# A WKV-scan block on one core: spreads and scans share one pool of eleven tiles, the decay's exponential moves from PSUM to SBUF, TensorE gets eight PSUM banks

## The chip, the cores and the metric

The kernel runs on one core of a Trainium2 chip. The metric is the device time of one execution in microseconds; several executions are timed and their median is the kernel's time. The core has five engines with a queue of instructions each: TensorE (PE; its weight loads are shown as PEld), VectorE (DVE), ScalarE (ACT), GpSimd (POOL) and SyncE (SP), which here issues most of the DMAs. Each engine works its own queue strictly in order, and semaphores hold an instruction until what it needs is done. SBUF is the large on-chip memory, PSUM the small one in which TensorE leaves its results; in this kernel GpSimd only ever reads and writes SBUF.

## What is computed

`x` has 8 batches of 256 tokens with 512 channels. Each batch goes through one recurrent block, all in float32:

```python
xn = ln(x); sx = shift(xn) - xn                                  # token shift
xxx = tanh((xn + sx * maa_x) @ maa_w1)                           # five small gates
x5  = xn + sx * (maa_stack + xxx @ maa_w2)                       # five mixed inputs
w = exp(-exp(time_decay + tanh(x5[1] @ decay_w1) @ decay_w2))
r, k, v = x5[3] @ Wr.T, x5[0] @ Wk.T, x5[2] @ Wv.T
g = silu(x5[4] @ Wg.T)
for t in tokens:                                                 # 32 heads of 16 x 16 state
    a = k_t[:, None] * v_t[None, :]
    out_t = r_t @ (u * a + s)
    s = a + w_t[:, None] * s
x = x + (groupnorm(out) * g) @ Wo.T
xn2 = ln2(x); sx2 = shift(xn2) - xn2
x = x + sigmoid(xr @ ffn_Wr.T) * (relu(xk @ ffn_Wk.T) ** 2 @ ffn_Wv.T)   # xk, xr from xn2, sx2
```

## The kernel before

Each batch has three stages: `inputs_of_scan` (layer norm, mixing, projections to r, k, v, g and the decay), `scan` (the recurrence) and `rest` (group norm, output projection and the second half). The stages of neighbouring batches are interleaved.

**The scan.** Channels are on the partitions, in 4 blocks of 128. A block's state has 16 columns per channel, worked in 4 groups of 4 columns, so there are 8 x 4 x 4 = 128 groups. Per block, ACT writes `wrep`, the decay exp(-w) repeated four times along time (L883). Per group:

1. a DMA on the SP queue spreads `v` rows from DRAM (`vo`) into a `vs` tile of 128 x 4 x 256 (L389, 512 KB);
2. ACT writes the initial state into column 0 (L893);
3. DVE multiplies `vs` in place by `k` (L900). The copy of `k` that it reads, `kp`, was put into PSUM by ACT. For 6 of the 128 groups POOL does this product instead (L897), reading `k` from SBUF;
4. DVE runs the recurrence along time with one TENSOR_TENSOR_SCAN of 1024 elements (L902): it reads `wrep` and `vs` and writes a tile `st` of a second pool, `st8`;
5. POOL multiplies `st` by `r`, in place (L905);
6. when four groups are done, PE sums them over the key index into a PSUM tile `pat` (L913), and DVE adds that to `att` (L919).

**Memory.** `vs` has 6 tiles and `st8` has 6, each 4 KB per partition, in SBUF. `wrep` is one tile in PSUM and takes two of its eight banks; the other six are the pool `ps`, through which every result of TensorE and the `kp` copies pass. In batch 0, before the first scan, two of the mixing results are put into `wrep`'s banks (`wide` in `mixed`), and DVE then sets its first column to zero again.

**Order.** Every operation is recorded with an engine and with the tiles that it reads and writes. `Plan.order` takes the operations by a written rank, the table `TURNS` (one number per operation, a row per batch and stage), gives each a tile from its pool and a planned start, and emits them by planned start. What comes out is a fixed order on each engine's queue. Plain products ("any") take the tiling of their neighbours on PE: four matmuls on 32 columns each, or one on 128 (`mul`, L400).

The two lines on which the change turns, with their operands:

```python
    w, pat = new("wrep", f"wrep{b}_{blk}"), new("ps", f"pat{b}_{blk}")
...
    dve(4 * T, [st], [w, vs], lambda w=w, vs=vs, st=st: nc.vector.tensor_tensor_scan(st(), w(), vs(), 0.0, ALU.mult, ALU.add), 2.085)
    gp(4 * T, st, [st, r], lambda m=m, st=st, r=r: nc.gpsimd.tensor_tensor(st(), st(), r()[:, m : m + 1, :].to_broadcast([P, 4, T]), ALU.mult), 1.815)
```

(shown with the reshaping of the scan's operands left out.)

Of the kernel before, what the change touches and what calls it, by code (L numbers as in the profile page):

```python
# [12 lines left out]
P = 128  # L13
# [54 lines left out]
class Plan:  # L68
# [46 lines left out]
    def stage(self):  # L115
# [224 lines left out]
def tile_rwkv_block(  # L340
# [98 lines left out]
    pool("att", 3, [P, 2 * T + 4])  # L439

    pool("vo", 3, [2, P, T], dram)
    pool("vs", 6, [P, 4, T])
    pool("rk", 2, [P, 2, T])
    pool("st8", 6, [P, 4, T])
    pool("sq", 2, [P, E])
    pool("x2", 2, [P, NT, E + 1])
    pool("o", 2, [P, E])
    pool("Ws", 4, [P, 2, E])
    pool("wrep", 1, [P, 4, T], pp)
    pool("ps", 6, [P, 2, T], pp)  # L450


    def col(name, k):
# [679 lines left out]
```

## Time and profile before

| what | value |
|---|---|
| median of 3 runs | 613.29 us (613.27 to 614.44) |
| the profiled execution | 613.54 us, of which the span of the instructions 611.7 us |
| PE busy | 599.6 us (98%) |
| DVE busy | 545.4 us (89%) |
| POOL busy | 522.3 us (85%) |
| ACT busy | 514.3 us (84%) |
| granted TensorE clock | 0.997 on average |

A row of the groups reads: line, engine, operation, what it writes <- what it reads, shapes and count, then busy time, the mean of one in ns, and the engine's idle time just before. In the timeline a row begins with the start and the duration in us, and ends with xN, the number of equal instructions merged. The waits say who sat idle, until which instruction ended, for how long in total, how many times, and the longest. In the view by windows each stretch has the busy time of every engine and in brackets the count.

### The profile page before, as it was taken

The numbers are of one execution on the slowest core, as the hardware profiler recorded it, in microseconds if no ns is written. First come the engines' busy times: TensorE is split into PE (matmuls) and PEld (weight loads), VectorE is DVE, ScalarE is ACT, GpSimd is POOL, SyncE is SP. The second block draws the span as 40 slices with busy tenths as digits, with TensorE's granted clock in tenths as the row PEclk, the third lists the DMA queues.
The fourth block names the chain that finished last, engine by engine and source line by source line (L and its number), as shares of the span: only waits on it lengthen the run. The fifth ranks groups of instructions, "written<-read, shape, count | busy, mean of one in ns | idle before, by whom it ended". The sixth has DMA issues, their size and how long they took to land.

```text
span 611.7 us, 17692 instructions
## 1 busy us (share of the span) xinstructions
PE 599.6 (98%) x7322; PEld 350.8 (57%) x7322; DVE 545.4 (89%) x489; ACT 514.3 (84%) x1172; POOL 522.3 (85%) x418
## 2 busy tenths in 40 slices
PE   8899999999999999999999999999999999999997
PEld 7576755657544764367553775455654464547464
DVE  6599999999999998899998999999999999996342
ACT  5797689999999999999999798999899789965450
POOL 2889999999899998889998999899999988978030
PEclk9899999999999999999999999999999999999999
DMA  9897777788858777958767687896786677971552
GB/s 289 276 234 170 193 185 209 193 211 195 240 157 232 195 197 234 280 137 243 198 194 213 193 249 188 207 288 165 194 244 168 186 220 208 268 227 33 186 164 91
DMA packets 52495, 124.76 MB, mean 204 GB/s; under 512 B 5824, under 2 KB 11200, under 8 KB 52416
## 3 DMA queue, kind: packets, MB, share of 16 engines
q1 hardware_dynamic: 47904, 119.39, 71.6%
q10 hardware_dynamic: 4512, 4.26, 2.2%
q8 instruction: 57, 0.93, 0.7%
q14 instruction: 22, 0.18, 0.1%
HBM read 115.25 MB, written 8.39 MB: 202 GB/s over the span
## 4 chain that ended last, share of the span: by engine, by line
PE 84%; ACT 5%; DVE 5%; POOL 3%; issue 1%; DMA 0%; ACTq 0%; DVEq 0%; POOLq 0%
PE ps L400 70%; PE ps L913 8%; PE ps L606 2%; PE ps L777 2%; POOL st L905 1%; ACT ps L720 1%; DVE st L902 1%; ACT rk L968 1%; ACT sq L968 1%; POOL g L979 1%; PE ps L855 1%; PE ps L939 0%; DMA xt<-in_x 0%; DVE mix L639 0%; DVE mix L722 0%
## 5 line engine op out<-in xcount | busy, mean ns | idle before, releaser
L902 DVE TENSOR_TENSOR_SCAN st<-wrep,vs 128x1024 f32<-128x1024 f32 x128 | 288.8, 2276 | 4.0 <-ACT wrep L883 2.1
L905 POOL TENSOR_TENSOR st<-st,r 128x1024 f32<-128x1024 f32 x128 | 254.2, 2003 | 11.7 <-DVE st L902 7.1
L900 DVE TENSOR_TENSOR vs<-vs,ps 128x1024 f32<-128x1024 f32 x122 | 143.5, 1207 | 3.0 <-ACT vs L893 3.0
L400 PE MATMUL ps<-Ws,mix 128*32 128x512 f32 (+2 forms) x864 | 115.4, 589 | 0.2 <-DVE o L1026 0.2
L400 PEld LDWEIGHTS ps<-Ws,mix 128*32 128x32 f32 (+1 forms) x864 | 37.6, 116 | 61.8 <-issue 55.7
L737 POOL TENSOR_TENSOR mix<-mix,xn 128x512 f32<-128x512 f32 x62 | 67.0, 1098 | 5.5 <-DVE mix L722 5.3
L400 PE MATMUL ps<-mix,Wv 128*32 128x256 f32 (+1 forms) x808 | 61.6, 381 | 1.8 <-DVE mix L734 1.8
L913 PE MATMUL ps<-st,con 128*32 128x256 f32 x1024 | 62.3, 380 | 0.1
L400 PE MATMUL ps<-mix,Wk 128*32 128x256 f32 (+1 forms) x904 | 60.0, 379 | 0.6 <-DVE mix L722 0.6
L400 PE MATMUL ps<-mix,Wg 128*32 128x256 f32 (+1 forms) x736 | 59.1, 380 | 0.2 <-DVE mix L722 0.2
L400 PE MATMUL ps<-mix,Wr 128*32 128x256 f32 (+1 forms) x712 | 59.0, 380 | 0.0
L400 PE MATMUL ps<-mix,Ws 128*32 128x256 f32 (+1 forms) x688 | 57.7, 379 | 0.5 <-issue 0.5
L400 PE MATMUL ps<-Ws,g 128*32 128x512 f32 (+1 forms) x428 | 56.8, 593 | 0.3 <-POOL g L979 0.2
L627 POOL TENSOR_TENSOR sx<-xn 128x512 f32<-128x512 f32 x31 | 32.3, 1050 | 28.3 <-ACT xn L622 23.6
L652 POOL TENSOR_TENSOR mix<-mix,xn 128x512 f32<-128x512 f32 x44 | 47.6, 1099 | 5.8 <-ACT mix L650 5.6
L400 PEld LDWEIGHTS ps<-mix,Wv 128*32 128x32 f32 (+1 forms) x808 | 39.5, 118 | 20.0 <-DVE mix L734 2.2
L400 PEld LDWEIGHTS ps<-mix,Ws 128*32 128x32 f32 (+1 forms) x688 | 40.5, 123 | 16.0 <-POOL st L905 0.8
L400 PEld LDWEIGHTS ps<-mix,Wk 128*32 128x32 f32 (+1 forms) x904 | 39.0, 113 | 18.1 <-issue 1.5
L400 PEld LDWEIGHTS ps<-mix,Wr 128*32 128x32 f32 (+1 forms) x712 | 39.7, 122 | 16.5 <-issue 1.0
L720 ACT ACTIVATE ps<-ps,vec 128x256 f32<-128x256 f32 x112 | 46.4, 444 | 3.1 <-PE ps L400 1.7
L863 ACT COPY att<-ps 32x256 f32<-32x256 f32 x128 | 46.5, 363 | 2.8 <-PE ps L855 0.7
L913 PEld LDWEIGHTS ps<-st,con 128*32 128x32 f32 x1024 | 32.7, 110 | 27.6 <-issue 5.5
(138 smaller groups left out, 976.5 us busy)
## 6 DMA issues: line engine op xcount, KB each, us to landing
vs<-vo SPq DMA_DIRECT2D x128, 512.0 KB, 5.6
Ws<-in_wo SPq DMA_DIRECT2D x16, 512.0 KB, 5.7
Ws<-in_fr SPq DMA_DIRECT2D x16, 512.0 KB, 5.7
Ws<-in_fk SPq DMA_DIRECT2D x16, 512.0 KB, 6.0
Ws<-in_fv SPq DMA_DIRECT2D x16, 512.0 KB, 5.1
x<-in_x SPq DMA_DIRECT2D x9, 512.0 KB, 6.0
vo<-v ACTq DMA_DIRECT2D x15, 256.0 KB, 5.9
out<-o SPq DMA_DIRECT2D x15, 256.0 KB, 4.7
```

Source lines behind the costliest of these rows:

```text
L400: nc.tensor.matmul(out[i : i + n], lhsT=w[:, i : i + n], rhs=x, start=first, stop=final)
L606: nc.tensor.transpose(ps()[:, m, n * P : (n + 1) * P], xh[n]()[:, k * P : (k + 1) * P], idt())
L627: take(512, [sx], [xn], lambda xn=xn, sx=sx, e=nc.vector if quick else nc.gpsimd: e.tensor_tensor(sx(), xn()[:, :, 0:T], xn()[:, :, 1 : T ...
L652: gp(512, t, [t, xn[q]], lambda q=q, t=t: nc.gpsimd.tensor_tensor(t(), t(), xn[q]()[:, :, 1 : T + 1], ALU.add))
L720: act(256, p_, [p_, vec], lambda g=g, q=q, m=m, p_=p_: nc.scalar.activation(p_()[:, m, :], p_()[:, m, :], AF.Identity, bias=col(f"maa_{g}" ...
L737: gp(512, t, [t, xn[q]], lambda q=q, t=t: nc.gpsimd.tensor_tensor(t(), t(), xn[q]()[:, :, 1 : T + 1], ALU.add))
L777: nc.tensor.matmul(pd()[i : i + 32, 0, :], lhsT=w, rhs=src[k // 2]()[:, k % 2, :], start=(k == begin), stop=(k == end))
L863: act(350, atts[q], [pc], lambda i=32 * (2 * q + m), m=m, q=q, h=32 * h: nc.scalar.copy(atts[q]()[h : h + 32, m, :], pc()[i : i + 32, 0, :]))
L900: dve(4 * T, [vs], [vs, kp], lambda m=m, vs=vs, kp=kp: nc.vector.tensor_tensor(vs(), vs(), kp()[:, m : m + 1, :].to_broadcast([P, 4, T]), ...
L902: dve(4 * T, [st], [w, vs], lambda w=w, vs=vs, st=st: nc.vector.tensor_tensor_scan(st().rearrange("p n t -> p (n t)"), w().rearrange("p n ...
L905: gp(4 * T, st, [st, r], lambda m=m, st=st, r=r: nc.gpsimd.tensor_tensor(st(), st(), r()[:, m : m + 1, :].to_broadcast([P, 4, T]), ALU.mul ...
L913: nc.tensor.matmul(pat()[32 * i : 32 * i + 32, 0, :], lhsT=con()[:, s : s + 32], rhs=done[i]()[:, j, :], start=(j == 0), stop=(j == 3),)
```

## The change

- `st8` goes. `vs` has eleven tiles instead of six, and the scan writes its result over its own input: `st` is the same tile as `vs`, from the landing of the spread to the sum on PE.
- `wrep` is still one tile, but in SBUF.
- `ps` has eight PSUM banks instead of six.
- Batch 0's mixing results all go to `ps`; `wide` and the DVE memset behind it go.
- `TURNS` has other numbers throughout, so every queue has another order. The operations are the same, one memset fewer. 16 products of 128 x 256 and 2 of 128 x 512 that PE did as four 32-column matmuls are now single 128-column ones.

```diff
     TURNS = """
-        1 118 15 38 54 77 67 76 58 75 96 64 90 111 2 20 144 166 167 168 31 19 36 35 48 56 33 53 66 32 46 47 34 37 49,
...
-    pool("vs", 6, [P, 4, T])
+    pool("vs", 11, [P, 4, T])
     pool("rk", 2, [P, 2, T])
-    pool("st8", 6, [P, 4, T])
...
-    pool("wrep", 1, [P, 4, T], pp)
-    pool("ps", 6, [P, 2, T], pp)
+    pool("wrep", 1, [P, 4, T], sb)
+    pool("ps", 8, [P, 2, T], pp)
...
             ps = {(g, q): new("ps", f"psm{b}_{g}_{q}") for g in groups for q in range(NQ)}
-            if b == 0:
-                wide = new("wrep", f"psm{b}")
-                ps.update({(g, 0): Part(wide, lambda t, i=i: t[:, 2 * i : 2 * i + 2, :]) for i, g in enumerate(groups[:2])})
...
-            if b == 0:
-                dve(4, [wide], [], lambda: nc.vector.memset(wide()[:, :, 0:1], 0.0))
             return x5
...
-                vs, st = (new(p_, f"{p_}{b}_{blk}_{i}") for p_ in ("vs", "st8"))
+                vs = st = new("vs", f"vs{b}_{blk}_{i}")
```

237 rows, old and new, of the table TURNS are left out of this document.

## The prediction

> **What bounds the kernel now.** I read the page's engine totals first, then the windows, to see which stretch the scans fill, and the groups in it.
>
> ```profile
> PE 599.6 (98%) x7322; PEld 350.8 (57%) x7322; DVE 545.4 (89%) x489; ACT 514.3 (84%) x1172; POOL 522.3 (85%) x418
> ```
> ```profile
> 0.00:34.00 34.00, 30.13 (x268) 22.67 (x269) 21.15 (x48) 22.89 (x56) 20.12 (x35) 0.95 0.89 277
> 34.00:562.00 528.00, 523.69 (x6868) 303.86 (x6870) 507.43 (x413) 472.70 (x1085) 494.99 (x378) 1.00 0.77 205
> 562.00:612.00 50.00, 45.82 (x196) 24.29 (x184) 16.78 (x30) 18.74 (x32) 7.19 (x7) 1.00 0.43 142
> ```
> ```profile
> L902 DVE TENSOR_TENSOR_SCAN st<-wrep,vs 128x1024 f32<-128x1024 f32 x128 | 288.8, 2276 | 4.0 <-ACT wrep L883 2.1
> L905 POOL TENSOR_TENSOR st<-st,r 128x1024 f32<-128x1024 f32 x128 | 254.2, 2003 | 11.7 <-DVE st L902 7.1
> L900 DVE TENSOR_TENSOR vs<-vs,ps 128x1024 f32<-128x1024 f32 x122 | 143.5, 1207 | 3.0 <-ACT vs L893 3.0
> ```
>
> The windows' columns are PE, PEld, DVE, ACT, POOL, clock, DMA. All scans lie in the middle stretch of 528 us. There PE is busy for 523.7 us and sets the pace, but DVE has only 20.6 us free and POOL 33.0 us. So the question for each part of the change is whether it lengthens DVE or POOL: POOL has 33.0/128 = 0.26 us to spare per scan, no more.
>
> **The decay's exponential in SBUF.** This decides the case. Before, the scan reads one tile from SBUF (`vs`) and one from PSUM (`wrep`); after, both from SBUF. First, how DVE and POOL get along now, from the views of `st`'s line and of the tile `wrep` (min/median/max in ns):
>
> ```profile
> L905 POOL TENSOR_TENSOR st<-st,r x128: 1990/2001/2027, 37.6 to 557.4; 128x1024 f32<-128x1024 f32 x128
> ```
> ```profile
> L902 DVE TENSOR_TENSOR_SCAN st<-wrep,vs x128: 2226/2279/2292, 35.2 to 555.1; 128x1024 f32<-128x1024 f32 x128
> ```
>
> Both engines are over 93% busy in the stretch, so nearly every scan runs beside a POOL product, and neither kind varies by more than 66 ns. They do not disturb each other. But at the start of batch 0, DVE runs a few operations that read two SBUF tiles, beside POOL. The timeline there (start, duration):
>
> ```profile
> 9.29 1.14 POOL L627 TENSOR_TENSOR sx<-xn 128x512 f32<-128x512 f32 x1 [4.44 <-ACT mix L616]
> 9.45 1.26 DVE L639 SCALAR_TENSOR_TENSOR mix<-xn,vec,mix 128x256 f32<-128x256 f32 x1
> 10.39 1.22 POOL L627 TENSOR_TENSOR sx<-xn 128x512 f32<-128x512 f32 x1
> 11.81 0.47 DVE L639 SCALAR_TENSOR_TENSOR mix<-xn,vec,mix 128x256 f32<-128x256 f32 x1
> 15.63 1.27 POOL L728 TENSOR_TENSOR mix<-mix,sx 128x512 f32<-128x512 f32 x1 [0.47 <-ACT mix L726]
> 15.78 1.66 DVE L734 TENSOR_TENSOR mix<-mix,xn 128x512 f32<-128x512 f32 x1
> 16.97 1.42 POOL L737 TENSOR_TENSOR mix<-mix,xn 128x512 f32<-128x512 f32 x1
> 18.26 0.69 DVE L734 TENSOR_TENSOR mix<-mix,xn 128x512 f32<-128x512 f32 x1
> 18.35 1.73 POOL L728 TENSOR_TENSOR mix<-mix,sx 128x512 f32<-128x512 f32 x1
> 21.21 3.19 POOL L737 TENSOR_TENSOR mix<-mix,xn 128x512 f32<-128x512 f32 x3
> ```
>
> The same DVE operation takes 0.47 us when POOL is idle (11.81) and 1.26 us when POOL started 0.16 us earlier (9.45): POOL ends at 10.43, DVE at 10.71. At 15.78 the product that takes 0.69 us alone (18.26) takes 1.66 and ends 0.55 us after POOL does. The other way round, POOL's 1.27 us become 1.73 when DVE was there first (18.35). They take turns, whole instruction by whole instruction. The scan is the one large DVE operation that the change puts into this class.
>
> The price, on POOL. Undisturbed, consecutive POOL products of 512 start (3.19 - 1.09)/2 = 1.05 us apart; 1.09 is the length of one:
>
> ```profile
> 27.29 1.09 POOL L737 TENSOR_TENSOR mix<-mix,xn 128x512 f32<-128x512 f32 x1
> ```
>
> With a DVE operation in between, the ends 10.43 and 11.61 are 1.18 apart: POOL lost 0.13 to an operation of 0.47. The starts 16.97 and 18.35 are 1.38 apart: it lost 0.33 to one of 0.69. So POOL loses the DVE operation's length less 0.34 to 0.36 where POOL was first, and 1.73 - 1.27 = 0.46 of 0.69, that is less 0.23, where DVE was first. POOL is busy 94% of the stretch, so it is mostly there first; I take 0.35: a scan costs POOL 2.276 - 0.35 = 1.93 us, 128 scans 247 us. The bounds are 2.276 - 0.36 = 1.92 (246 us) and the whole scan (291 us).
>
> The Trainium skill, "SBUF — State Buffer", section "Who interferes with whom", says that a VectorE instruction with two SBUF inputs contends with a GpSimd instruction that reads SBUF, that the second to issue is held until the first has finished, and that one with a single SBUF input is free of this. The rows above agree for both kinds, but none shows a scan with two SBUF inputs. By that section of the Trainium skill the whole 2.276 us would be lost each time, and the sum below would come to 905 us.
>
> On DVE, a scan that finds POOL at work waits for the rest of its product, and longer products are met more often. The large products are the 128 of L905 and these 6, and ten groups of 512 elements have 229 between them, of which these are the first and the last:
>
> ```profile
> L897 POOL TENSOR_TENSOR vs<-vs,k 128x1024 f32<-128x1024 f32 x6 | 13.2, 2200 | 0.0
> L737 POOL TENSOR_TENSOR mix<-mix,xn 128x512 f32<-128x512 f32 x62 | 67.0, 1098 | 5.5 <-DVE mix L722 5.3
> L728 POOL TENSOR_TENSOR mix<-mix,sx 128x512 f32<-128x512 f32 x2 | 3.0, 1498 | 0.5 <-ACT mix L726 0.5
> ```
>
> With 134 products of about 2.0 us and 229 of about 1.09 us in POOL's 522 us, the mean rest is (134 x 2.0² + 229 x 1.09²)/(2 x 522) = 0.77 us; 128 of them make 99 us. DVE then has 507 + 99 = 606 us of work and waiting, while POOL has 495 + 247 = 742. POOL becomes the bound, and DVE's wait is covered by it. Without that cover it would cost up to 99 us (below). Behind a waiting scan in DVE's queue stand the `vs` products and the mixing products that feed POOL again.
>
> Whether a scan itself is quicker from SBUF: DVE's 512-element product takes 678 ns with an operand in PSUM and 692 ns from SBUF. I take no difference; 14 ns x 128 = 2 us of DVE either way.
>
> ```profile
> L722 DVE TENSOR_TENSOR mix<-ps,sx 128x512 f32<-128x512 f32 x56 | 36.3, 678 | 4.3 <-ACT ps L720 3.0 <-issue 1.1
> L977 DVE TENSOR_TENSOR g<-att,g 128x512 f32<-128x512 f32 x2 | 1.4, 692 | 0.9 <-ACT att L974 0.9
> L720 ACT ACTIVATE ps<-ps,vec 128x256 f32<-128x256 f32 x112 | 46.4, 444 | 3.1 <-PE ps L400 1.7
> L650 ACT ACTIVATE mix<-sx,vec 128x256 f32<-128x256 f32 x88 | 40.2, 503 | 3.9 <-POOL sx L627 3.2 <-DVE sx L627 0.4
> ```
>
> ACT writes `wrep` 32 times; between PSUM and SBUF its 256-element operations differ by 59 ns, so 2 us more or less in all on an engine with 55 us free in the stretch: nothing. `wrep` stays a single tile, so DVE's 2.1 us of waiting for it (L902's row) stays too.
>
> **One pool of eleven.** No instruction is added. A tile is now held from the issue of its DMA to the sum on PE.
>
> ```profile
> SPq L389 <- DVE st L902: 238.9, 83, 8.7
> ```
>
> The DMA queue waits for a free tile most of its waiting time, but it has room: 6 + 6 tiles over 128 groups in 528 us allow 6 x 528/128 = 24.8 us in `vs` and as much in `st8`, at most 49.5 us together. Eleven tiles in a stretch of 757 us allow 11 x 757/128 = 65 us. So I cost it at nothing. At the old pace it would be 45 us, perhaps tight; that cover comes from the slower pace itself. Behind a late spread in SP's queue stand weight loads, for PE, which has time.
>
> **Eight banks.** PE's idle time in the stretch is 4.3 us, so at most that could be won if PE still set the pace. With POOL as the bound it is worth nothing. The dropped memset is 0.06 us of DVE in the first stretch, and the regrouped products are PE work that POOL's pace covers.
>
> **New turns.** The same work in another order: what it can give POOL is idle time between 0 and the present 33.0 us. Most of that idle time ends with ACT or DVE, which now run ahead, so I take 15 us, about half. The first and last stretch hold no scan. The last is the chain of batch 7 with PE at 45.8 of 50 us, so I keep 34 and 50 us.
>
> **The sum.** 34 + (495 + 247 + 15) + 50 = 841 us of span. The profiled execution had 613.54 us around a span of 611.7, so 1.8 us go on top: 843 us. It stands 0.25 us above the median of the three runs, which changes nothing. The bounds give 34 + 495 + 246 + 50 + 2 = 827 and 34 + 495 + 291 + 33 + 50 + 2 = 905.
>
> **The rivals.**
> - *Not slower: a scan does not take turns with POOL.* No row shows a scan with two SBUF inputs. Then PE stays the bound and the two banks may close its gaps: 613.5 - 4.3 = 609 us. It decides if a scan costs POOL less than 0.26 us. Against it: both kinds of two-input operations that the trace shows were held by whole instructions.
> - *Half.* The scan spends 2276 ns on 1024 elements where the product (L900) spends 1207, so its reading may leave room for POOL every other time. Half of 1.93 us is 0.97, 124 us in all: 34 + 495 + 124 + 15 + 50 + 2 = 720 us. Against it: the DVE operation at 9.45 got in only after POOL's end, in no gap.
> - *DVE's waits come back to POOL.* If what stands behind the waiting scans is what POOL needs next, the 99 us are not covered: 843 + 99 = 942 us. It decides once DVE's waits pass (742 - 507)/128 = 1.84 us per scan, close to POOL's longest product; so it is unlikely in full.
>
> **How the numbers follow.** The forecast has 0.79, the half 0.07, DVE's waits 0.07, no turns 0.06; 0.01 is left over. Predicted: 843 us. The likeliest case's own range is 827 to 905. The range of 785 to 945 adds the case of DVE's waits and an error in the idle time on the other side; it leaves out the half, no turns, and some 0.05 of tails, under 0.2. Faster by over 0.2% (about what this kernel's runs can tell from no change): 0.05, within: 0.01, slower: 0.94.
>
> **What would show it.** POOL: busy time up by about 247 us to near 770, its 1024-element products spread from 2.0 to over 4 us, and the longest chain through POOL and DVE. DVE: scans at about 2.28 + 0.77 = 3.0 us on average with a wide spread, L900 still at 1.2. PE: busy near 72% of the span, its clock still near 1.0 in the stretch. The prediction is wrong if scans stay at 2.28 with POOL's products at 2.00, if POOL is idle for over 60 us in the stretch, or if the first or last stretch moves by more than 10 us.

## The result, and the profile after

The changed kernel takes 842.37 us (842.16 to 842.79, 4 runs) where the kernel before takes 613.28 us beside it: 1.375 times as long, with a 95% interval of 1.373 to 1.377. Forecast were 843 us.

Engine totals after, then the same three stretches by windows (PE, PEld, DVE, ACT, POOL, clock, DMA), then the two groups that answer to those of before:

```profile
PE 674.2 (80%) x7214; PEld 368.9 (44%) x7214; DVE 645.0 (77%) x488; ACT 518.2 (62%) x1172; POOL 764.7 (91%) x418
```
```profile
0.00:34.00 34.00, 31.20 (x250) 23.81 (x251) 21.59 (x46) 24.19 (x58) 21.12 (x35) 1.00 0.89 276
34.00:790.00 756.00, 596.73 (x6770) 320.47 (x6772) 606.18 (x413) 474.69 (x1082) 737.05 (x378) 0.90 0.54 143
790.00:841.00 51.00, 46.23 (x204) 24.62 (x196) 17.19 (x30) 19.32 (x33) 6.58 (x7) 0.99 0.41 139
```
```profile
L896 DVE TENSOR_TENSOR_SCAN vs<-wrep,vs 128x1024 f32<-128x1024 f32 x128 | 386.4, 3041 | 10.3 <-ACT wrep L877 8.9
L899 POOL TENSOR_TENSOR vs<-vs,r 128x1024 f32<-128x1024 f32 x128 | 335.0, 2633 | 5.0 <-DVE vs L896 4.9
L894 DVE TENSOR_TENSOR vs<-vs,ps 128x1024 f32<-128x1024 f32 x122 | 144.6, 1203 | 56.0 <-ACT vs L887 33.3
```

Three things are to be seen. The number of instructions is the same on POOL (418) and nearly so elsewhere, but POOL is busy for 242 us more. The middle stretch holds all but 1 us of the growth, 528 to 756 us, and in it POOL has 737 us of work and waiting, DVE 606, PE 597: the bound has gone from PE to POOL. And the scans and POOL's products got longer, while DVE's product with an operand in PSUM (L894) did not, at 1203 ns.

The minimum, median and maximum in ns of the two groups, by their lines, tell how:

```profile
L896 DVE TENSOR_TENSOR_SCAN vs<-wrep,vs x128: 2256/3034/4409, 32.7 to 777.3; 128x1024 f32<-128x1024 f32 x128
L899 POOL TENSOR_TENSOR vs<-vs,r x128: 1988/2002/4067, 36.9 to 786.2; 128x1024 f32<-128x1024 f32 x128
```

The quickest scan takes 30 ns more from SBUF than it did with PSUM (minimum 2256, before 2226), and the quickest POOL product is as quick as ever (1988, before 1990). They are long when they meet. The chain that ended last says where the time is:

```profile
POOL 72%; PE 10%; issue 8%; ACT 6%; DVE 3%; ACTq 0%; POOLq 0%; DVEq 0%
```

And the timeline in mid-kernel shows the turns (start, duration):

```profile
419.51 1.03 POOL L626 TENSOR_TENSOR sx<-xn 128x512 f32<-128x512 f32 x1
420.02 2.67 DVE L896 TENSOR_TENSOR_SCAN vs<-wrep,vs 128x1024 f32<-128x1024 f32 x1
420.50 3.02 POOL L626 TENSOR_TENSOR sx<-xn 128x512 f32<-128x512 f32 x1
422.61 3.06 DVE L896 TENSOR_TENSOR_SCAN vs<-wrep,vs 128x1024 f32<-128x1024 f32 x1
423.48 3.98 POOL L899 TENSOR_TENSOR vs<-vs,r 128x1024 f32<-128x1024 f32 x1
```

The scan whose row starts at 420.02 ends at 422.69, 2.15 us after the POOL operation that ends at 420.54: it waited for that one. POOL's next, which took 1.03 us in the row before, takes 3.02 and ends at 423.52, after the scan. The row of the second scan starts at 422.61, and it ends at 425.67, again 2.15 us after POOL's operation; POOL's product of 2.0 us that stands behind it takes 3.98.

### The profile page after: what moved, and what is told of

Read it like the earlier page. It is cut to its first block, busy times and chain, and to the rows that moved or that the text cites. A ratio compares the mean times of both kernels' runs of the same rounds, so it can differ in the third digit from the quotient of the medians.

```text
span 840.7 us, 17431 instructions
## 1 busy us (share of the span) xinstructions
PE 674.2 (80%) x7214; PEld 368.9 (44%) x7214; DVE 645.0 (77%) x488; ACT 518.2 (62%) x1172; POOL 764.7 (91%) x418
## 4 chain that ended last, share of the span: by engine, by line
POOL 72%; PE 10%; issue 8%; ACT 6%; DVE 3%; ACTq 0%; POOLq 0%; DVEq 0%
POOL vs L899 29%; POOL mix L733 11%; PE ps L400 7%; POOL mix L651 7%; POOL sx L626 5%; POOL mix L759 3%; POOL rs L585 2%; POOL rk L844 2%; POOL att L964 2%; POOL o L1025 2%; POOL rs L552 2%; POOL vs L891 2%; POOL att L863 2%; POOL g L973 2%; DVE vs L896 1%
## 5 line engine op out<-in xcount | busy, mean ns | idle before, releaser
L896 DVE TENSOR_TENSOR_SCAN vs<-wrep,vs 128x1024 f32<-128x1024 f32 x128 | 386.4, 3041 | 10.3 <-ACT wrep L877 8.9
L899 POOL TENSOR_TENSOR vs<-vs,r 128x1024 f32<-128x1024 f32 x128 | 335.0, 2633 | 5.0 <-DVE vs L896 4.9
L894 DVE TENSOR_TENSOR vs<-vs,ps 128x1024 f32<-128x1024 f32 x122 | 144.6, 1203 | 56.0 <-ACT vs L887 33.3
L907 PE MATMUL ps<-vs,con 128*32 128x256 f32 x1024 | 86.3, 443 | 51.4 <-POOL vs L899 50.5
L733 POOL TENSOR_TENSOR mix<-mix,xn 128x512 f32<-128x512 f32 x62 | 104.6, 1704 | 1.4 <-DVE mix L718 1.3
L400 PE MATMUL ps<-mix,Wv 128*32 128x256 f32 (+1 forms) x688 | 71.7, 448 | 17.4 <-POOL mix L733 13.6
L626 POOL TENSOR_TENSOR sx<-xn 128x512 f32<-128x512 f32 x31 | 53.2, 1723 | 32.5 <-ACT xn L621 27.2
L907 PEld LDWEIGHTS ps<-vs,con 128*32 128x32 f32 x1024 | 38.1, 123 | 94.1 <-POOL vs L899 62.1
L649 ACT ACTIVATE mix<-sx,vec 128x256 f32<-128x256 f32 x88 | 41.2, 501 | 51.0 <-POOL sx L626 50.5
L651 POOL TENSOR_TENSOR mix<-mix,xn 128x512 f32<-128x512 f32 x44 | 69.6, 1595 | 1.5 <-ACT mix L649 1.5
L400 PE MATMUL ps<-mix,Wg 128*32 128x256 f32 (+1 forms) x736 | 70.0, 412 | 0.8 <-POOL mix L759 0.8
L400 PEld LDWEIGHTS ps<-mix,Wg 128*32 128x32 f32 (+1 forms) x736 | 45.1, 132 | 21.2 <-issue 6.1
```

The lines of the kernel that those rows point to most:

```text
L400: nc.tensor.matmul(out[i : i + n], lhsT=w[:, i : i + n], rhs=x, start=first, stop=final)
L626: take(512, [sx], [xn], lambda xn=xn, sx=sx, e=nc.vector if quick else nc.gpsimd: e.tensor_tensor(sx(), xn()[:, :, 0:T], xn()[:, :, 1 : T ...
L649: act(256, t, [sx[q], vec], lambda q=q, m=m, t=t: nc.scalar.activation(t()[:, m, :], sx[q]()[:, m, :], AF.Copy, scale=col(by, 2 * q + m)), ...
L651: gp(512, t, [t, xn[q]], lambda q=q, t=t: nc.gpsimd.tensor_tensor(t(), t(), xn[q]()[:, :, 1 : T + 1], ALU.add))
L733: gp(512, t, [t, xn[q]], lambda q=q, t=t: nc.gpsimd.tensor_tensor(t(), t(), xn[q]()[:, :, 1 : T + 1], ALU.add))
L894: dve(4 * T, [vs], [vs, kp], lambda m=m, vs=vs, kp=kp: nc.vector.tensor_tensor(vs(), vs(), kp()[:, m : m + 1, :].to_broadcast([P, 4, T]), ...
```

## The experiments

The theory: the scan with two SBUF inputs and POOL's operations take turns, and this makes the whole step. The rivals: the shared pool of eleven tiles, the new ranks or the eight banks make it; or the scan is slow from SBUF by itself.

**In place alone.** The kernel before with one part of the change:

```diff
-    pool("vs", 6, [P, 4, T])
+    pool("vs", 11, [P, 4, T])
-    pool("st8", 6, [P, 4, T])
...
-                vs, st = (new(p_, f"{p_}{b}_{blk}_{i}") for p_ in ("vs", "st8"))
+                vs = st = new("vs", f"vs{b}_{blk}_{i}")
```

> The kernel before with one part of the change: eleven tiles for spreads and scans, in place; the decay's exponential stays in PSUM, six banks, the old ranks. Theory (a scan with two SBUF inputs and POOL take turns): no scan has two SBUF inputs here, so scans stay at 2.28 us, POOL's products at 2.00, POOL's busy time at 522, and the time is 613 us, up to 625 if eleven tiles are tight at this pace. Rival (the shared pool holds the spreads back and this starves POOL): towards 842 us, with POOL idle.

619.69 us, 1.011 times before (1.008 to 1.014). Scans took 2278 ns, POOL's products 2003 ns, POOL was busy for 522.5 us:

```profile
PE 600.6 (97%) x7322; PEld 348.3 (57%) x7322; DVE 545.2 (88%) x489; ACT 514.4 (83%) x1172; POOL 522.5 (85%) x418
L901 DVE TENSOR_TENSOR_SCAN vs<-wrep,vs 128x1024 f32<-128x1024 f32 x128 | 289.0, 2278 | 4.3 <-ACT wrep L882 3.2
```

So the pool costs 1.1% at PE's pace and nothing like 842.

**The exponential in SBUF on top of it.** The `wide` tile keeps its own two banks, so that TensorE has the six it had:

```diff
-    pool("wrep", 1, [P, 4, T], pp)
+    pool("wrep", 1, [P, 4, T], sb)
+    pool("wide", 1, [P, 4, T], pp)
...
-                wide = new("wrep", f"psm{b}")
+                wide = new("wide", f"psm{b}")
```

> The same, and the decay's exponential in SBUF; the old ranks, six banks for TensorE. Theory: this alone makes the step; POOL busy 765 us, scans 3.0 us on average, 842 us give or take 15. Rival (the new order or the two banks make it): as without the SBUF copy, 613 to 625 us. Rival (DVE's waits come back to POOL): 900 us and more.

838.73 us, 1.369 times before (1.365 to 1.373). From 619.69 to 838.73 by the place of one tile, with POOL's, DVE's and SP's queues in the same order:

```profile
PE 673.0 (80%) x7322; PEld 364.1 (43%) x7322; DVE 647.5 (77%) x489; ACT 517.5 (62%) x1172; POOL 764.1 (91%) x418
L902 DVE TENSOR_TENSOR_SCAN vs<-wrep,vs 128x1024 f32<-128x1024 f32 x128 | 388.8, 3056 | 11.6 <-ACT wrep L883 10.6
```

POOL is busy for 764.1 us, as in the changed kernel (764.7). The new ranks and two more banks are not needed for the step; they change 838.73 into 842.37.

**Half of it.** In place again, with the six banks and the old ranks. Blocks 1 and 3 of each batch have their exponential in SBUF, in a tile of its own (`wsb`), blocks 0 and 2 in PSUM (the edit is shown without the part that makes the scan work in place, and without the first column of `wsb` being set to zero):

```diff
+    pool("wsb", 1, [P, 4, T], sb)
...
-            w, pat = new("wrep", f"wrep{b}_{blk}"), new("ps", f"pat{b}_{blk}")
+            w, pat = new("wsb" if blk % 2 else "wrep", f"wrep{b}_{blk}"), new("ps", f"pat{b}_{blk}")
```

> In place, and only blocks 1 and 3 of each batch have their exponential in SBUF, so 64 of the 128 scans read two SBUF tiles. Theory: POOL loses 1.9 us to each of the 64, 122 us; with the old stretches 34 and 50, POOL's 495 and 19 us of idle time that is 34 + 495 + 122 + 19 + 50 + 2 = 722 us, POOL busy about 644. Rival (any such scan upsets the order of the whole, whatever their number): 800 us and more. Rival (PE's or DVE's slack hides the first half): under 690 us.

731.01 us, 1.194 times before (1.190 to 1.197). Both kinds of scan stand side by side in one kernel:

```profile
L902 DVE TENSOR_TENSOR_SCAN vs<-wsb,vs 128x1024 f32<-128x1024 f32 x64 | 191.3, 3011 | 3.0 <-ACT wsb L883 2.7
L902 DVE TENSOR_TENSOR_SCAN vs<-wrep,vs 128x1024 f32<-128x1024 f32 x64 | 144.7, 2278 | 3.7 <-ACT wrep L883 2.8
```

Those from SBUF wait 0.73 us on average, the others not at all. POOL was busy for 638.8 us, 116 us over the kernel before: 1.82 us for each of the 64 scans. With all 128 it is 242 us, 1.89 each. The price goes with the number of scans. The time is 9 us over the 722 that were expected.

**The changed kernel without the second SBUF input.** Everything of the change stays, ACT's exponential into SBUF too, but the scan reads one element of the copy of k in PSUM in its place:

```diff
-                dve(4 * T, [st], [w, vs], lambda w=w, vs=vs, st=st: nc.vector.tensor_tensor_scan(
-                    st().rearrange("p n t -> p (n t)"), w().rearrange("p n t -> p (n t)"),
-                    vs().rearrange("p n t -> p (n t)"), 0.0, ALU.mult, ALU.add), 2.085)
+                dve(4 * T, [st], [w, vs, kp], lambda m=m, kp=kp, vs=vs, st=st: nc.vector.tensor_tensor_scan(
+                    st().rearrange("p n t -> p (n t)"), kp()[:, m, 0:1].to_broadcast([P, 4 * T]),
+                    vs().rearrange("p n t -> p (n t)"), 0.0, ALU.min, ALU.add), 2.085)
```

> The changed kernel with eight banks, eleven tiles and the new ranks, and ACT still writes the decay's exponential into SBUF; only the scan reads one element of the copy of k in PSUM in its place, min for times (so the decay is left out, and the result is not the reference's). Each scan then has one SBUF input and the same 1024 elements. Theory (turns between scan and POOL make the whole step): scans 2.28, POOL's products 2.00 us, POOL busy 522, time 600 to 625 us. Rival (the new ranks are poor by themselves, as the 769 us with the exponential back in PSUM and six banks may suggest): 700 to 770 us, without any stretched product.

628.2 us, 1.024 times before (1.022 to 1.027), 3 us over what was expected.

```profile
PE 602.8 (96%) x7214; PEld 348.4 (56%) x7214; DVE 545.1 (87%) x488; ACT 515.6 (82%) x1172; POOL 522.2 (83%) x418
```
```profile
L896 DVE TENSOR_TENSOR_SCAN vs<-ps,vs 128x1024 f32<-128x1024 f32 x128 | 288.4, 2277 | 0.9
L899 POOL TENSOR_TENSOR vs<-vs,r 128x1024 f32<-128x1024 f32 x128 | 254.4, 2003 | 11.5 <-DVE vs L896 9.0 <-PE ps L400 1.7 <-DVE cm L837 0.2
```

POOL's busy time is back at 522 and the bound is back at PE. Of the 229 us of the change, 842.37 - 628.2 = 214 go with the place of the scan's second input. The other 15 us, 2.4%, are what eleven tiles, eight banks and the new ranks cost while PE sets the pace. (The copy of k lives longer here, which may move operations of PE and ACT; on POOL, DVE and SP the order is that of the changed kernel. So the 15 us are not exact.)

**Another operation in the same class.** In the kernel before, DVE's products by k read k from SBUF; the copy in PSUM is still made:

```diff
-                        vs(), vs(), kp()[:, m : m + 1, :].to_broadcast([P, 4, T]), ALU.mult))
+                        vs(), vs(), k.place[:, m : m + 1, 1 : T + 1].to_broadcast([P, 4, T]), ALU.mult))
```

> The kernel before, where DVE's 122 products of the spread tiles by k read k from SBUF and not its copy in PSUM (which is still made). The scans keep their PSUM operand. Theory (any DVE operation with two SBUF inputs takes turns with POOL, and costs POOL its length less some 0.4 us): 122 x (1.207 - 0.4) = 98 us on POOL, 34 + 495 + 98 + 19 + 50 + 2 = 698 us, give or take 12. Rival (it is a matter of the scan alone): 613 us.

720.81 us, 1.175 times before (1.173 to 1.177). It is not a matter of the scan: these products now wait in their turn and the scans do not.

```profile
L902 DVE TENSOR_TENSOR_SCAN st<-wrep,vs 128x1024 f32<-128x1024 f32 x128 | 288.6, 2274 | 6.3 <-POOL st L905 2.0 <-issue 1.2 <-ACT wrep L883 0.7
L900 DVE TENSOR_TENSOR vs<-vs,k 128x1024 f32<-128x1024 f32 x122 | 249.2, 2072 | 4.3 <-ACT vs L893 3.7 <-ACT k L808 0.6
```

The size was missed, 721 for 698 (give or take 12). POOL's busy time rose by 637.9 - 522.3 = 116 us, 0.95 us for a product of 1.207: it lost the length less 0.26 us, not less 0.4. That is 18 of the 23 us.

**POOL relieved.** The changed kernel, with POOL's product by r on the first column of each sequence only:

```diff
-                    st(), st(), r()[:, m : m + 1, :].to_broadcast([P, 4, T]), ALU.mult), 1.815)
+                    st()[:, :, 0:1], st()[:, :, 0:1], r()[:, m : m + 1, 0:1].to_broadcast([P, 4, 1]), ALU.mult), 1.815)
```

> The changed kernel with POOL's product by r cut to the first column of each sequence (4 elements for 1024), so most of that product is left out and the result is not the reference's. Scans keep two SBUF inputs. Theory (POOL is the bound because it has to wait for the scans): POOL's own work falls by about 230 us to 290, with 128 x 1.85 = 237 us of waiting it has some 530 us, less than PE's 600, and the time falls back to PE's pace, 615 to 650 us; scans, meeting POOL at work less often, fall from 3.04 to some 2.5 us. Rival (a scan from SBUF is slow by itself, and DVE is the bound): scans stay at 3.04 us, and the time stays over 750 us.

682.99 us, 1.113 times before (1.111 to 1.115). The rival falls: with the same inputs in SBUF the scans now take 2.61 us, and the kernel is 159 us quicker for work taken from POOL. But it did not go back to PE's pace, and this expectation was wrong:

```profile
L896 DVE TENSOR_TENSOR_SCAN vs<-wrep,vs 128x1024 f32<-128x1024 f32 x128 | 330.9, 2608 | 6.1 <-ACT wrep L877 4.7
L899 POOL TENSOR_TENSOR vs<-vs,r 128x4 f32<-128x4 f32 x128 | 76.2, 610 | 58.6 <-DVE vs L896 54.8 <-ACT vs L887 2.9
```

A product of four elements takes 0.61 us on average, 0.20 in the median and up to 2.24, and POOL is idle for 55 us until a scan is done. POOL is busy for 475 of 680 us, PE for 620, DVE for 588: no engine is full. That the time then goes into waits that pass from engine to engine is a reading of these numbers, not shown by a run.

**Putting the exponential back.** The changed kernel with `wrep` in PSUM, which leaves six banks:

```diff
-    pool("wrep", 1, [P, 4, T], sb)
-    pool("ps", 8, [P, 2, T], pp)
+    pool("wrep", 1, [P, 4, T], pp)
+    pool("ps", 6, [P, 2, T], pp)
```

> The changed kernel with the exponential back in PSUM, so six banks: eleven tiles in place and the new ranks stay. Theory: back to PE's pace, 613 us plus what ranks cost that were not made for six banks: 612 to 650 us, scans 2.28, POOL's products 2.00 us. Rival (the new order makes the step): near 842 us.

769.45 us, 1.257 times before (1.252 to 1.263), far from the 612 to 650 that were expected, and yet scans took 2279 ns, POOL's products 2002, and POOL was busy for 523.4 us. So this run is long for another reason. To tell which, the kernel with the scan's operand in PSUM was run with six banks instead of eight (`pool("ps", 6, ...)`, its only difference from the run of 628.2 us):

> As after_scan_psum (new ranks, eleven tiles, exponential written to SBUF, the scan reads an element of the copy of k in PSUM, so the decay is left out), but with six banks in place of eight. It tells what made the 769 us with the exponential back in PSUM. If the new ranks with only six banks give a poor order: 740 to 790 us, with scans at 2.28 and POOL's products at 2.00 us. If it was the exponential in PSUM itself: near 628 us.

799.88 us, 1.306 times before (1.301 to 1.310), against 628.2 with eight, and 10 us above the range that was expected for a poor order. No product is stretched here either (scans 2277 ns, POOL's products 2002):

```profile
PE 655.9 (82%) x7490; PEld 366.0 (46%) x7490; DVE 549.0 (69%) x488; ACT 518.5 (65%) x1172; POOL 523.8 (66%) x418
```

The new ranks and the eight banks belong together: with two banks fewer, the same ranks leave every engine idle for 143 us or more of 799 us, and PE does 276 more matmuls (7490 for 7214).

**One tile more.** In place, with twelve tiles (`pool("vs", 12, ...)`), exponential in PSUM, old ranks:

> inplace_eleven with a twelfth tile: as many tiles in one pool as the kernel before has in two, exponential in PSUM, old ranks, six banks. If the 619.7 us of eleven come from a tile too few: 613 us or a little less. If they come from holding spreads until PE's sum, or from the order that follows: 617 to 621 us.

614.82 us, 1.003 times before (1.002 to 1.005). Most of the 1.1% of eleven tiles was the missing tile. No variant was quicker than the kernel before.

## Why the prediction was right

| term | predicted | measured |
|---|---|---|
| what 128 scans cost POOL | 247 us (1.93 each) | 764.7 - 522.3 = 242 us (1.89 each) |
| POOL's idle time in the middle stretch | 15 us | 756 - 737 = 19 us |
| first and last stretch | 34 + 50 us | 34 + 51 us |
| DVE's work and waits in the stretch | 606 us | 606 us |
| a scan's mean | 3.0 us (2.28 + 0.77) | 3.04 us |
| span | 841 us | 840.7 us |

The step that carried it was to price the change on POOL and not on DVE, from ten rows of the first 25 us. The rule that those rows gave for two kinds of operation holds for the scan, by whole instructions: the half rival (720 us) and the one without turns (609 us) fall. The Trainium skill, "SBUF — State Buffer", section "Who interferes with whom", is borne out for the scan too; by its letter, with the scan's whole length lost, the sum would have been 34 + 495 + 291 + 15 + 50 + 2 = 887 us (the 905 us that the prediction gives for it also keep all 33 us of POOL's idle time). POOL lost 0.39 us less than the 2.28 each time. That part is no constant: it was 0.26 us for the products by k, and 0.23 to 0.36 in the prediction's rows. The rival in which DVE's waits come back to POOL (942 us) falls as well: DVE waited about as long as worked out, and POOL was idle for 19 us all the same.

Eleven tiles, eight banks and new ranks at no cost: right in the sum, since 838.73 without the last two becomes 842.37 with them, and only through the cover that was named. At PE's pace the pool costs 1.1%, as "perhaps tight" allowed, and all three together some 15 us.

Wrong was what the prediction said of PE: busy near 72% and a clock near 1.0. PE was busy for 80%, and its clock in the stretch was 0.90. A tenth of 756 us is 76 us, about the 73 us by which PE's busy time in the stretch grew (597 for 524), so the clock alone would explain it; that is an estimate. A narrow matmul, as in the sums of the scan, took 443 ns where it took 380 before (the sums' group after, and before):

```profile
L907 PE MATMUL ps<-vs,con 128*32 128x256 f32 x1024 | 86.3, 443 | 51.4 <-POOL vs L899 50.5
```
```profile
L913 PE MATMUL ps<-st,con 128*32 128x256 f32 x1024 | 62.3, 380 | 0.1
```

It cost little, as PE no longer set the pace: POOL was idle for only 19 us of the stretch, whatever it waited for. Wrong too was that the longest chain would run through POOL and DVE: POOL has 72% of it and DVE 3%, for the time in which a scan holds POOL lies in POOL's own lengthened rows.

That the total fell within 1 us is partly luck: the 247 us were 5 too many, the idle time 4 too few, and the bounds had been 827 to 905. The same reasoning missed by 23 us for the products by k and by over 30 us for the kernel with little work on POOL.

## What to carry to other kernels

Before an operand moves from PSUM to SBUF, look whether the DVE operation that reads it then has two SBUF inputs while POOL works: here that turned a PE-bound kernel into a POOL-bound one, at 1.9 us per scan. Search the trace for any small place where such operations already run beside each other; ten rows there gave the price to 2%. And try such a move without retuned ranks first: ranks made for eight banks cost up to 172 us with six (628.2 to 799.88), which hides what a single part does.

## What the runs showed of the hardware that had not been expected

Tiny operations are held as well: a POOL operation on two elements that takes 0.19 us alone took 2.06 beside a scan, and ended with it.

```profile
26.08 0.19 POOL L553 TENSOR_SCALAR rs<-mv 128x2 f32<-128x2 f32 x1 [0.68 <-ACT xh L551]
```
```profile
397.15 3.12 DVE L896 TENSOR_TENSOR_SCAN vs<-wrep,vs 128x1024 f32<-128x1024 f32 x1
398.19 2.06 POOL L552 TENSOR_SCALAR rs<-mv 128x2 f32<-128x2 f32 x1
```

(The first row is of the kernel before, the other two of the kernel after.) The eleven operations of this line take 0.19 us each when the scan of the changed kernel has its operand in PSUM, and 2.05 us in the median in the changed kernel.

And the granted TensorE clock was lower in the runs in which PE was busy for less of the span, with one small exception: 0.997 at 98% busy (before), 0.992 at 96% (scan with PSUM operand), 0.972 at 91% (POOL relieved), 0.966 and 0.946 at 88% (k from SBUF, half of the scans), 0.935 at 84% (exponential back in PSUM), 0.916 at 82% (scan with PSUM operand, six banks), 0.918 and 0.908 at 80% (in place with the exponential in SBUF, the changed kernel). What PE waited for in the changed kernel, with the total, the number and the longest wait in us:

```profile
PE ps L907 <- POOL vs L899: 50.5, 22, 5.0
PE ps L605 <- ACT xh L589: 22.2, 10, 7.3
PE ps L400 <- POOL mix L733: 21.8, 8, 7.1
```

The Trainium skill, "TensorE: Matmul & The Clock Gate", section "HAM oscillation — how this bites in real kernels", says that gaps of more than about 3.4 us on PE let its clock fall. The waits of up to 5.0, 7.3 and 7.1 us and the clock of 0.90 agree with it in direction. But the run with k from SBUF shows that shorter waits can be followed by a lower clock too: PE's longest wait between 30 and 93.5 us was 2.9 us, and the granted clock was 1.00 from 85 to 93.45 us and 0.50 in the 3.4 us from 93.5 on. No run here changes such a gap alone.
